# Expert stages of a macaron transformer kernel: three weight sets loaded ahead, five pinned behind the first tile, one-hots by fours

## The chip, the cores and the metric

The kernel runs on one core of one Trainium2 chip. The metric is device microseconds of that core for one execution of the whole program. The engines are named as the profile names them: PE (TensorE, matmuls; PEld is its weight load), DVE (VectorE), ACT (ScalarE), POOL (GpSimd), SP (SyncE, used for issuing DMAs). A name with a q behind it (PEldq, DVEq) stands for what the engine's sequencer does by itself: register loads, semaphore waits, DMA issues.

## The reference

The program is two layers over 1024 tokens of width 512. Cut to what matters here:

```python
h = layernorm(x)                               # 1024 tokens x 512
logits = h @ W_gate + b_gate                   # 8 experts
top2 = the two largest of the 8 logits         # per token
y = sum over its two experts e of
        0.25 * relu(h @ W_e[e] + b_e[e])       # mean of the two, times 0.5
x = x + y
x = x + attention(layernorm(x))                # 32 heads, causal
x = x + y of the same kind                     # expert stage, second time
x = x + 0.5 * lora_ffn(layernorm(x))           # 4 low-rank experts, top 1
x = x + mamba(layernorm(x))                    # 64 heads, state space scan
x = x + 0.5 * lora_ffn(layernorm(x))
```

The expert stage stands twice in the program, once ahead of the attention (called f0) and once after it (f1), with the same weights. Everything is float32, but for the one-hot matrices of the routing, which are bfloat16.

## The kernel before, in words

The tokens lie in eight tiles of 128 (NT = 8). An expert stage is the function `expert_ffn(tag, before_rows, meanwhile, behind_weights)`. It has four parts.

**Loads.** `w_all` (eight experts of 1 MB, 128 partitions by 4 by 512) and `b_all` (eight bias rows, each broadcast over the partitions) are loaded by SP: four experts, their four biases, four experts, their four biases. Then the callback `behind_weights` runs; f0 passes none, in f1 it is the loader of small arrays of the mamba (`par.load`). The loads that follow on SP in f0 are those of the attention's first head group: `w_v`, four of `w_q`, `w_k`, `w_o`. The normalized tokens are written to a DRAM array `rows`, so that they can be gathered.

**Routing.** Logits, the two chosen experts, and for each (token, choice) pair a position `pos` in a list that is ordered by expert and padded to whole tiles of 128 for each expert: NS = 23 slot tiles in the worst case. `ends` says in which slot tile each expert ends. DVE does nearly all of it. Sixteen one-hot matrices `at_row` (128 x 128, line 442) times `what` give, summed on PE into `ps_slot` (line 445), the token of every slot; `lane_of` and `token` (lines 453 and 455) turn this into indices. Apart from that, `past_e` (line 485), two steps `of_f` and the cast `of_i` (line 495) make the number of the expert that each slot tile belongs to, and two casts `slot_i` (line 497) hold where each token finds its two results.

**Slot tiles.** For each of 23 tiles: POOL gathers 128 rows (`xs`, line 463, an indirect DMA that is issued two tiles ahead, from three buffers); PE transposes it (`ps_tr`, line 156) and ACT copies the result (`xt_s`, line 477); PE multiplies it with the weights of one expert (`ps_e`, line 510); DVE adds the bias (`y_e`, line 518), ACT does the relu and issues the store. Which expert it is, is known to the chip alone, so that both PE and DVE read the number from `of_i` into a register:

```python
low, high = max(0, s - (NS - NE)), min(s, NE - 1)
ep = nc.tensor.value_load(of_i[0:1, s : s + 1], min_val=low, max_val=high)   # L506
ev = nc.vector.value_load(of_i[0:1, s : s + 1], min_val=low, max_val=high)   # L507
```

The bound `high` also means that the product of tile s needs the weights of experts 0 to s at most.

**Work beside it.** In f0, POOL makes what the first head group of the attention needs: `w_q` is scaled in two halves (line 659), and four sums and differences of halves of `w_q` and `w_k` (function `sums`, line 636) are formed.

The order of instructions on each engine is not that of the text alone: a scheduler orders them by their dependences, and `tc.keep_in_program_order` pins an instruction to its place in the text. Behind the expert stages, pipelines over the tiles (`Tiles`) run a list of steps, one tile behind the other; a `None` in the list is an empty step, by which the later steps of a tile come one round later. `Lora.steps` is such a list: normalize, transpose, None, gate, choose, turn (which makes `zt`), None, finish.

Of the kernel before, what the change touches and what calls it, by code (L numbers as in the profile page):

```python
# [13 lines left out]
F32 = mybir.dt.float32  # L14
# [4 lines left out]
ALU = mybir.AluOpType  # L19
# [3 lines left out]
P = 128  # L23
# [3 lines left out]
KT = D // P  # L27
# [6 lines left out]

NE = 8
NS = 2 * S // P + NE - 1
NE1 = 4
RANK = 8

# [36 lines left out]
def macaron_kernel(  # L76
# [23 lines left out]
    nc = tc.nc  # L100

    const = ctx.enter_context(tc.tile_pool(name="const", bufs=1))
# [6 lines left out]
    rows = dram.tile([S, D], F32, tag="rows", name="rows")  # L109
    outs = dram.tile([NS * P, D], F32, tag="outs", name="outs")  # L110

# [5 lines left out]

    x = const.tile([P, NT, D], F32, tag="x", name="x")
    hT = const.tile([P, KT, S], F32, tag="hT", name="hT")
    x_src = x_in.rearrange("(t p) d -> p t d", p=P)  # L120
    for t in range(NT):
        (nc.sync, nc.scalar)[t % 2].dma_start(x[:, t, :], x_src[:, t, :])
# [8 lines left out]
    for e in range(NE):  # L131
        nc.gpsimd.memset(rank8[:, e : e + 1], float(NE - e))

    gate_w = const.tile([P, KT, NE], F32, tag="gate_w", name="gate_w")
    nc.scalar.dma_start(gate_w, w_gate.rearrange("(k p) e -> p k e", p=P))
    gate_b = const.tile([P, NE], F32, tag="gate_b", name="gate_b")
    nc.scalar.dma_start(gate_b, b_gate.partition_broadcast(P))
    lg = const.tile([P, NT, NE], F32, tag="lg", name="lg")
    slot = [
        const.tile([P, NT], U32, tag=f"slot{i}", name="slot_i") for i in range(2)  # L140
    ]
# [156 lines left out]
    def expert_ffn(tag, before_rows, meanwhile, behind_weights=lambda: None):  # L298
# [5 lines left out]
        with tc.tile_pool(name=f"{tag}wa", bufs=1) as wap, tc.tile_pool(  # L304
            name=f"{tag}r", bufs=1
        ) as rp, tc.tile_pool(name=f"{tag}w", bufs=3) as wk:
            w_all = wap.tile([P, NE, KT, D], F32, tag="w_all", name="w_all")
            b_all = wap.tile([P, NE, D], F32, tag="b_all", name="b_all")
            for e in range(NE):
                nc.sync.dma_start(  # L310
                    w_all[:, e, :, :], w_e[e].rearrange("(k p) c -> p k c", p=P)
                )
                if e % 4 == 3:
                    for b in range(e - 3, e + 1):
                        nc.sync.dma_start(b_all[:, b, :], b_e[b].partition_broadcast(P))
            behind_weights()


            lanes = rp.tile([P, P], F32, tag="lanes", name="lanes")
            steps = rp.tile([P, NS + 1], F32, tag="steps", name="steps")  # L320
            counts = rp.tile([P, P], I32, tag="counts", name="counts")
            nc.gpsimd.iota(counts, pattern=[[1, P]], base=0, channel_multiplier=0)
            nc.gpsimd.tensor_copy(lanes, counts)
            nc.gpsimd.tensor_scalar(steps, lanes[:, : NS + 1], float(P), None, ALU.mult)
            lane = rp.tile([P, 1], F32, tag="lane", name="lane")
# [63 lines left out]
            ends = rp.tile([P, NE], F32, tag="ends", name="ends")  # L389
# [14 lines left out]
            pos = rp.tile([P, 2, NT], F32, tag="pos", name="pos")  # L404
            for i, sel in enumerate((sel1, sel2)):
# [7 lines left out]
            flat = pos.rearrange("p i t -> p (i t)")  # L413
            past = rp.tile([P, n2, NS + 1], F32, tag="past", name="past_s")
            nc.vector.tensor_tensor(
                past,
                flat.unsqueeze(2).to_broadcast([P, n2, NS + 1]),
                steps.unsqueeze(1).to_broadcast([P, n2, NS + 1]),
                ALU.is_ge,
# [3 lines left out]
            row_of = rp.tile([P, n2], F32, tag="row_of", name="row_of")  # L423
# [15 lines left out]
            at_row = rp.tile([P, n2, P], BF16, tag="at_row", name="at_row")  # L439
            ps = psml.tile([P, 512], F32, tag="ps", name="ps_slot")  # L440
            for j in range(n2):
                nc.vector.tensor_scalar(
                    at_row[:, j, :], lanes, row_of[:, j : j + 1], None, ALU.is_equal
                )
                nc.tensor.matmul(
                    ps[:, : 2 * NS],
                    lhsT=at_row[:, j, :],
                    rhs=what[:, j, :, :].rearrange("p i s -> p (i s)"),
                    start=(j == 0),
                    stop=(j == n2 - 1),  # L450
                )
# [21 lines left out]
            def turn(s):  # L473
                xs = gathered.pop(s)
                ps = transposes(lambda i: xs[:, i * P : (i + 1) * P], KT)
                xt = wk.tile([P, KT, P], F32, tag="xt", name="xt_s")
                nc.scalar.copy(xt.rearrange("p k c -> p (k c)"), ps)
                turned[s] = xt

            for s in range(2):  # L480
# [1 line left out]


            past = rp.tile([P, NS, NE], F32, tag="past_e", name="past")
            nc.vector.tensor_tensor(
                past,
                ends.unsqueeze(1).to_broadcast([P, NS, NE]),
                lanes[:, :NS].unsqueeze(2).to_broadcast([P, NS, NE]),
                ALU.is_le,
            )  # L490
            of = rp.tile([P, NS], F32, tag="of", name="of_f")
            nc.vector.tensor_reduce(of, past, AX.X, ALU.add)
# [1 line left out]
            of_i = rp.tile([P, NS], I32, tag="of_i", name="of_i")  # L494
            nc.vector.tensor_copy(of_i, of)
            for i in range(2):
                nc.vector.tensor_copy(slot[i], pos[:, i, :])
            turn(0)
            for s in range(NS):
                if s + 2 < NS:  # L500
                    gather(s + 2)
                if s + 1 < NS:
                    turn(s + 1)
                xt = turned.pop(s)
# [3 lines that stand above are left out]
                ps = psml.tile([P, 512], F32, tag="ps", name="ps_e")  # L508
                for k in range(KT):
                    nc.tensor.matmul(  # L510
                        ps,
                        lhsT=xt[:, k, :],
                        rhs=w_all[:, bass.ds(ep, 1), k, :].rearrange("p e c -> p (e c)"),
                        start=(k == 0),
                        stop=(k == KT - 1),
                    )
                y = wk.tile([P, D], F32, tag="y", name="y_e")
                nc.vector.tensor_tensor(
                    y,
                    ps,  # L520
                    b_all[:, bass.ds(ev, 1), :].rearrange("p e c -> p (e c)"),
                    ALU.add,
                )
                nc.scalar.activation(y, y, AF.Relu, scale=0.25)
                nc.scalar.dma_start(outs[s * P : (s + 1) * P, :], y)
                if s > 3 and s % 2 == 0 and meanwhile:
                    meanwhile.pop(0)()
# [3 lines left out]
    def collect(make):  # L531


        def f(t):
            pair = pairs[t] = make()
            for i in range(2):
                tc.keep_in_program_order(
                    nc.gpsimd.indirect_dma_start(
                        out=pair[:, i, :],
                        out_offset=None,  # L540
                        in_=outs,
                        in_offset=bass.IndirectOffsetOnAxis(
                            ap=slot[i][:, t : t + 1], axis=0
                        ),
                        bounds_check=NS * P - 1,
                        oob_is_err=True,
                    )
                )

        return f  # L550
# [7 lines left out]
    class Lora:  # L558


        def __init__(self, pool):
            self.store = False
            self.pool = pool
            self.nz = NE1 * RANK
            self.lg_w = pool.tile([P, KT, self.nz + NE1], F32, tag="lg_w", name="lg_w")
            nc.scalar.dma_start(self.lg_w, lora_gate_t.rearrange("(k p) c -> p k c", p=P))
            self.lb_w = pool.tile([self.nz, D], F32, tag="lb_w", name="lb_w")
            nc.scalar.dma_start(self.lb_w, lora_b)
            self.ebias = pool.tile([P, NE1], F32, tag="ebias", name="ebias")
            nc.scalar.dma_start(self.ebias, exp_bias.partition_broadcast(P))  # L570
# [5 lines left out]
        def gate(self, t):  # L576
            narrow_by_columns(t, self.lg_w, self.nz + NE1)

        def choose(self, t):
            nz = self.nz  # L580
            ps = narrow_by_rows(t, nz + NE1)
            lg = self.pool.tile([P, 1, NE1], F32, tag="lg", name="lg1")
            nc.vector.tensor_tensor(lg[:, 0, :], ps[:, nz : nz + NE1], self.ebias, ALU.add)
# [29 lines left out]
        def steps(self):  # L613
            return (
                normalize,
                transpose_h,
                None,
                self.gate,
                self.choose,
                self.turn,  # L620
                None,
                self.finish,
            )
# [43 lines left out]
    def attention(left, causal, first, after):  # L667
        with tc.tile_pool(name="a_v", bufs=2) as vp, tc.tile_pool(
            name="a_qk", bufs=2
        ) as qkp, tc.tile_pool(name="a_p", bufs=3) as pp, tc.tile_pool(  # L670
            name="a_pt", bufs=1
        ) as ptp, tc.tile_pool(name="a_o", bufs=5) as op, tc.tile_pool(
            name="a_s", bufs=5
# [10 lines left out]
                both = pp.tile([P, S], F32, tag="pr", name="pair")  # L684
                return both.rearrange("p (i d) -> p i d", i=2)

            Tiles(collect(pair), None, None, add_pair, transpose_h, None, first_v).flush()


            b11, b12 = hT[:, :2, :512], hT[:, :2, 512:]  # L690
# [316 lines left out]
    def mamba(lora, par):  # L1007
        conv, dsk, nwt, w_dt, dtb, av = par.conv, par.dsk, par.nwt, par.w_dt, par.dtb, par.av
        nct = MI // P
        with ExitStack() as ms:  # L1010
# [13 lines left out]
            with tc.tile_pool(name="m_dt", bufs=1) as dp, tc.tile_pool(  # L1024
                name="m_pair", bufs=3
# [77 lines left out]
                def add_bias(t):  # L1103
# [7 lines left out]
                Tiles(  # L1111
                    collect(pair),
                    None,
                    None,
                    add_pair,
                    *lora.steps()[1:],
                    normalize,
# [360 lines left out]
```

## Time and profile before

| what | value |
|---|---|
| median of 3 runs | 2932.33 us (2929.51 to 2936.05) |
| the profiled execution | 2935.3 us, its span 2933.6 us |
| mean granted clock of PE | 0.978 |
| busy: PE, PEld, DVE, ACT, POOL | 95%, 54%, 60%, 24%, 31% of the span |
| f0 | first bn_stats at 4.34, first gather issued at 43.13, first transpose of a tile at 50.09, last product about 143.5 |
| attention | about 148 to 1605 |
| f1 | routing on DVE from 1613.25, first gather issued at 1628.08, first transpose at 1632.78, last product about 1725 |
| LoRA, mamba, LoRA | 1729 to 2933 |

Times in rows of the profile are microseconds from the start of the span unless marked ns. In a row of the timeline stand the start, the duration, the engine, the line, the operation, output and inputs by their names, the shape, how many instructions of the kind were joined, and in brackets how long the engine had stood idle before it and what ended this. "issue" is time in which the engine waited for nothing that the profile shows, for example because its sequencer was at work on instructions that are not counted as busy.

### The profile page before, as it was taken

Reading aid. Unit: us, or ns where it says so; the run is one execution under the profiler, and the core shown is the slowest. Engines: PE = TensorE matmul, PEld = TensorE weight load, DVE = VectorE, ACT = ScalarE, POOL = GpSimd, SP = SyncE. Lnnn points to the kernel's source line nnn. Section 1 sums busy time; section 2 is a strip of 40 time slices with the busy share of each in tenths; the row PEclk is TensorE's granted clock in tenths of the full one; section 3 lists DMA queues with packets and bytes.
Section 4 is the critical chain, followed back from the end, with each engine's and each line's share of the span. In section 5 each row is a group of like instructions: output and inputs, shape, how many; then the busy total and the mean of one; then the engine's idle time right before and its main releaser. Section 6 shows DMA issues by size and latency. Waiting matters only on the chain.

```text
span 2933.6 us, 30294 instructions
## 1 busy us (share of the span) xinstructions
PE 2800.9 (95%) x11051; PEld 1587.3 (54%) x11051; DVE 1745.8 (60%) x3239; ACT 709.4 (24%) x1381; POOL 898.8 (31%) x733
## 2 busy tenths in 40 slices
PE   5979999999999999999999769899999999999989
PEld 3435666656666666666654334454555555555544
DVE  3146555665656656556564234777776777767673
ACT  1212212231212222212222222422222232222320
POOL 4231112121122212112100230255554545455450
PEclk8989999999999999999999889999999999999999
DMA  8420001010010001001015340233232222223210
GB/s 297 126 72 29 15 15 44 1 44 15 15 44 15 29 15 43 15 15 43 1 36 194 101 122 18 83 101 108 86 108 94 86 98 97 93 87 122 87 44 29
DMA packets 102178, 196.99 MB, mean 67 GB/s; under 512 B 9040, under 2 KB 34800, under 8 KB 102032
## 3 DMA queue, kind: packets, MB, share of 16 engines
q1 hardware_dynamic: 84896, 157.15, 16.1%
q0 software_dynamic: 6240, 20.45, 2.7%
q10 hardware_dynamic: 10896, 17.47, 1.6%
q8 instruction: 89, 1.46, 0.2%
q14 instruction: 57, 0.47, 0.1%
HBM read 176.17 MB, written 18.87 MB: 66 GB/s over the span
## 4 chain that ended last, share of the span: by engine, by line
PE 84%; DVE 6%; POOL 4%; issue 3%; DMA 2%; ACT 0%; POOLq 0%; DVEq 0%; SPq 0%; ACTq 0%
PE ps_in L230 15%; PE ps_m L912 13%; PE ps_o L732 8%; PE ps_s L708 8%; PE ps_tr L156 7%; PE ps_out L1360 6%; PE ps_m L884 6%; PE ps_wo L821 6%; PE ps_e L510 5%; PE ps_y L1308 3%; PE ps_up L241 2%; PE ps_st L1326 1%; DVE xc L1161 1%; DVE e_seg L1265 1%; PE ps_v L241 1%
## 5 line engine op out<-in xcount | busy, mean ns | idle before, releaser
L708 PE MATMUL ps_s<-kT,qT 128*128 128x512 f32 (+3 forms) x768 | 292.8, 488 | 0.1
L732 PE MATMUL ps_o<-pT,v 128*128 128x512 f32 (+3 forms) x768 | 260.4, 489 | 0.0
L753 ACT COPY pT<-ps_tr 128x256 f32<-128x256 f32 (+2 forms) x192 | 91.7, 478 | 647.3 <-PE ps_tr L156 635.5
L722 ACT ACTIVATE pr<-ps_s,nm 128x128 f32<-128x128 f32 (+7 forms) x256 | 190.3, 744 | 238.3 <-DVE nm L719 207.9
L1360 PE MATMUL ps_out<-w_out,yg 128*128 128x512 f32 x512 | 241.1, 615 | 3.0 <-DVE yg L1323 3.0
L230 PE MATMUL ps_in<-hT,w_g 128*128 128x512 f32 x512 | 227.1, 596 | 8.2 <-issue 8.2
L1290 POOL TENSOR_TENSOR cs<-cT,dd 128x1024 f32<-128x1024 f32 x56 | 184.2, 3289 | 161.6 <-PE ps_y L1308 138.8
L230 PE MATMUL ps_in<-hT,w_x 128*128 128x512 f32 x512 | 225.8, 593 | 0.0
L732 PEld LDWEIGHTS ps_o<-pT,v 128*128 128x128 f32 x768 | 144.3, 191 | 145.6 <-issue 99.9
L719 DVE TENSOR_REDUCE nm<-ps_s 128x1 f32<-128x128 f32 (+7 forms) x256 | 192.2, 752 | 3.9
L156 PEld LDWEIGHTS ps_tr<-ident,pr 128*128 128x128 f32 x1152 | 136.9, 142 | 76.1 <-issue 44.8
L156 PE MATMUL ps_tr<-ident,pr 128*128 128x128 f32 x1152 | 171.4, 276 | 4.5 <-DVE pr L724 3.2
L510 PE MATMUL ps_e<-w_all,xt_s 128*128 (+1 forms) x368 | 168.1, 601 | 0.0
L724 DVE TENSOR_SCALAR pr<-pr,sm 128x128 f32<-128x128 f32 (+7 forms) x256 | 162.9, 637 | 7.7 <-DVE sm L723 0.5
L230 PEld LDWEIGHTS ps_in<-hT,w_g 128*128 128x128 f32 x512 | 96.6, 190 | 127.8 <-issue 127.8
L230 PEld LDWEIGHTS ps_in<-hT,w_x 128*128 128x128 f32 x512 | 97.0, 190 | 120.9 <-issue 120.4
L1265 DVE TENSOR_TENSOR_SCAN e_seg<-dd,eye 128x1024 f32<-128x1024 f32 x64 | 152.3, 2380 | 7.7 <-PE ps_y L1308 5.8
L1161 DVE SCALAR_TENSOR_TENSOR xc<-ps_in,conv,xc 128x511 f32<-128x511 f32 (+2 forms) x192 | 141.5, 737 | 17.9 <-ACT xc L1157 17.6
L708 PEld LDWEIGHTS ps_s<-kT,qT 128*128 128x128 f32 x768 | 127.5, 192 | 39.8 <-issue 26.8
L1360 PEld LDWEIGHTS ps_out<-w_out,yg 128*128 128x128 f32 x512 | 94.5, 195 | 98.4 <-issue 98.4
L806 POOL TENSOR_TENSOR so<-oT 128x256 f32<-128x256 f32 x28 | 20.0, 726 | 380.2 <-DVE oT L739 336.7
L1284 POOL TENSOR_TENSOR xw<-xdt,erev 128x512 f32<-128x512 f32 x56 | 58.4, 1043 | 251.6 <-DVE xdt L1278 195.0
(271 smaller groups left out, 4759.2 us busy)
## 6 DMA issues: line engine op xcount, KB each, us to landing
dd<-decay SPq DMA_DIRECT2D x128, 512.0 KB
w_all<-in_w_e_dram SPq DMA_DIRECT2D x16, 1024.0 KB
outs<-y_e ACTq DMA_DIRECT2D x46, 256.0 KB
w_v<-in_wkv_dram SPq DMA_DIRECT2D x8, 1024.0 KB
w_q<-in_wq_dram SPq DMA_DIRECT2D x32, 256.0 KB
w_k<-in_wkv_dram SPq DMA_DIRECT2D x8, 1024.0 KB
w_o<-in_wo_dram SPq DMA_DIRECT2D x8, 1024.0 KB
w_x<-in_in_wt_dram SPq DMA_DIRECT2D x8, 1024.0 KB
```

Of the source, the lines that this page charges most:

```text
L156: nc.tensor.transpose(ps[:, i * P : (i + 1) * P], src(i), ident)
L230: nc.tensor.matmul(ps[:, cols : cols + n], lhsT=w[:, k, c0 : c0 + P], rhs=hT[:, k, t0 : t0 + n], start=(k == 0), stop=(k == KT - 1),)
L510: nc.tensor.matmul(ps, lhsT=xt[:, k, :], rhs=w_all[:, bass.ds(ep, 1), k, :].rearrange("p e c -> p (e c)"), start=(k == 0), stop=(k == KT - 1),
L708: nc.tensor.matmul(ps[:, j : j + m], lhsT=qT[:, qt * P : (qt + 1) * P], rhs=kT[:, j : j + m], start=True, stop=True,)
L719: nc.vector.tensor_reduce(nm, ps[:, :n], AX.X, ALU.max, negate=True)
L722: nc.scalar.activation(pr[:, :n], ps[:, :n], AF.Exp, bias=nm, accum_out=sm)
L732: nc.tensor.matmul(ps[:, lo:512], lhsT=v[:, kb, hh * P : (hh + 1) * P], rhs=pT[:, kb, lo:512], start=(kb == 0), stop=(kb == last),)
L821: nc.tensor.matmul(ps[:, j, :], lhsT=lf[i][k][:, j * P : (j + 1) * P], rhs=rt[i][:, k, :], start=(first and j == 0 and k == 0), stop=(k == 1),
L912: nc.tensor.matmul(ps, lhsT=gr["left"][i][:, k, hh * P : (hh + 1) * P], rhs=right[i][:, k, :], start=(first and k == 0), stop=(last and k ...
L1265: nc.vector.tensor_tensor_scan(e.rearrange("p h l -> p (h l)"), dd[:, 0, :], eye8.rearrange("p h l -> p (h l)"), 0.0, ALU.mult, ALU.add,)
L1290: nc.gpsimd.tensor_tensor(cs, un["cT"][:, tok].unsqueeze(1).to_broadcast([P, HPG, P]), dd[:, 1, :].rearrange("p (h l) -> p h l", l=P), ALU ...
L1360: nc.tensor.matmul(po, lhsT=yg[:, k, :], rhs=w_o[:, k, :], start=(k == 0), stop=(k == 3))
```

## The change

The changed kernel does the following.

1. The loads of `gate_w` and `gate_b` stand ahead of the loads of x on ACT's queue; before, they stood behind.
2. SP loads the weights of three experts (NF = 3), then all eight biases. The weights of the other five experts are loaded from ACT's queue; these loads are pinned behind the transposes and the copy of slot tile 0 (`turn(0)`). The callback `behind_weights` is called twice, behind the first loads and behind the second.
3. The sixteen one-hots are made by four instructions of 128 x 512 in place of sixteen of 128 x 128.
4. `past_e` and the two casts `slot_i` are pinned to their place in the text, behind the first two gathers.
5. `Lora.steps` has one more empty step ahead of `turn`; the step lists of the attention and of the mamba have one fewer.

```diff
+NF = 3
...
+    gate_w = const.tile([P, KT, NE], F32, tag="gate_w", name="gate_w")
+    nc.scalar.dma_start(gate_w, w_gate.rearrange("(k p) e -> p k e", p=P))
+    gate_b = const.tile([P, NE], F32, tag="gate_b", name="gate_b")
+    nc.scalar.dma_start(gate_b, b_gate.partition_broadcast(P))
     x_src = x_in.rearrange("(t p) d -> p t d", p=P)
...
-    gate_w = const.tile([P, KT, NE], F32, tag="gate_w", name="gate_w")
-    nc.scalar.dma_start(gate_w, w_gate.rearrange("(k p) e -> p k e", p=P))
-    gate_b = const.tile([P, NE], F32, tag="gate_b", name="gate_b")
-    nc.scalar.dma_start(gate_b, b_gate.partition_broadcast(P))
...
+            def load_expert(eng, e):
+                return eng.dma_start(
+                    w_all[:, e, :, :], w_e[e].rearrange("(k p) c -> p k c", p=P)
+                )
+
+            for e in range(NF):
+                load_expert(nc.sync, e)
             for e in range(NE):
-                nc.sync.dma_start(
-                    w_all[:, e, :, :], w_e[e].rearrange("(k p) c -> p k c", p=P)
-                )
-                if e % 4 == 3:
-                    for b in range(e - 3, e + 1):
-                        nc.sync.dma_start(b_all[:, b, :], b_e[b].partition_broadcast(P))
+                nc.sync.dma_start(b_all[:, e, :], b_e[e].partition_broadcast(P))
             behind_weights()
...
             for j in range(n2):
-                nc.vector.tensor_scalar(
-                    at_row[:, j, :], lanes, row_of[:, j : j + 1], None, ALU.is_equal
-                )
+                if j % 4 == 0:
+                    four = [P, 4, P]
+                    nc.vector.tensor_tensor(
+                        at_row[:, j : j + 4, :],
+                        lanes.unsqueeze(1).to_broadcast(four),
+                        row_of[:, j : j + 4].unsqueeze(2).to_broadcast(four),
+                        ALU.is_equal,
+                    )
...
-            nc.vector.tensor_tensor(
-                past,
-                ends.unsqueeze(1).to_broadcast([P, NS, NE]),
-                lanes[:, :NS].unsqueeze(2).to_broadcast([P, NS, NE]),
-                ALU.is_le,
+            tc.keep_in_program_order(
+                nc.vector.tensor_tensor(
+                    past,
+                    ends.unsqueeze(1).to_broadcast([P, NS, NE]),
+                    lanes[:, :NS].unsqueeze(2).to_broadcast([P, NS, NE]),
+                    ALU.is_le,
+                )
             )
...
             for i in range(2):
-                nc.vector.tensor_copy(slot[i], pos[:, i, :])
+                tc.keep_in_program_order(nc.vector.tensor_copy(slot[i], pos[:, i, :]))
             turn(0)
+            for e in range(NF, NE):
+                tc.keep_in_program_order(load_expert(nc.scalar, e))
+            behind_weights()
             for s in range(NS):
...
                 self.gate,
                 self.choose,
+                None,
                 self.turn,
...
-            Tiles(collect(pair), None, None, add_pair, transpose_h, None, first_v).flush()
+            Tiles(collect(pair), None, add_pair, transpose_h, None, first_v).flush()
...
                 Tiles(
                     collect(pair),
                     None,
-                    None,
                     add_pair,
                     *lora.steps()[1:],
```

More of the change, by code (lines that the diff above doesn't have):

```diff
@@ L308, in expert_ffn @@
             b_all = wap.tile([P, NE, D], F32, tag="b_all", name="b_all")
-            for e in range(NE):
-                nc.sync.dma_start(
+            def load_expert(eng, e):
+                return eng.dma_start(
                     w_all[:, e, :, :], w_e[e].rearrange("(k p) c -> p k c", p=P)
                 )
-                if e % 4 == 3:
-                    for b in range(e - 3, e + 1):
-                        nc.sync.dma_start(b_all[:, b, :], b_e[b].partition_broadcast(P))
+            for e in range(NF):
+                load_expert(nc.sync, e)
+            for e in range(NE):
+                nc.sync.dma_start(b_all[:, e, :], b_e[e].partition_broadcast(P))
             behind_weights()
```

## The prediction

> **What bounds the kernel now.** I read first the page's busy shares, then the chain of waits inside the two expert stages, then the timeline and the windows there, because all edits lie in those stages.
>
> ```profile
> PE 2800.9 (95%) x11051; PEld 1587.3 (54%) x11051; DVE 1745.8 (60%) x3239; ACT 709.4 (24%) x1381; POOL 898.8 (31%) x733
> ...
> L510 PE MATMUL ps_e<-w_all,xt_s 128*128 (+1 forms) x368 | 168.1, 601 | 0.0
> ```
>
> TensorE (PE) is busy 95% of the span: whatever makes PE stand still is paid in full, and of its 133 us of idleness 58 lie in the two expert stages (f0 from 0 to 148 us: 38; f1 from 1605 to 1633: 20) and 26 behind the second (1726 to 1765). Its L510 groups run without gaps once begun (idle 0.0). Second, the chain of waits in f1:
>
> ```profile
> 1611.27 16.57 issue
> 1627.84 0.03 POOLq L463
> 1627.87 0.21 issue
> 1628.08 3.50 DMA xs<-rows,token
> 1631.58 1.20 issue
> 1632.78 1.96 PE ps_tr L156 x8
> ```
>
> The rows of the first tile had landed at 1631.58, yet PE began only at 1632.78. The "issue" of 1.20 us is PE's own sequencer, and the rows of line 506 (`value_load` of `of_i` on PE) in that stretch say what it did:
>
> ```profile
> L506 PEldq TENSOR_LOAD <-of_i x18: 296/299/307, 1620.3 to 1632.1; - x18
> L506 PEldq FUSED_REGOPS  x18: 146/146/151, 1620.7 to 1632.5; - x18
> L506 PEldq SEQ_ASSERT  x18: 18/18/18, 1620.9 to 1632.7; - x18
> ```
>
> Each register load is three sequencer instructions. 18 of them fill 1620.3 to 1632.7, so one takes 12.4 / 18 = 0.69 us (0.30 + 0.15 + 0.02, the rest between them). They are executed in program order with the matmuls. Before the change they cost little because they stand where PE waits for routing and gathers anyway. DVE pays the same price: the 13.93 us "issue" before the first `y_e` below are such loads, and nobody on PE waits for it.
>
> Third, f0 in the timeline:
>
> ```profile
> 43.13 1.27 POOL L463 DMA_INDIRECT xs<-rows,token  x1 [25.85 <-DMA b_all<-in_b_e_dram]
> ...
> 50.09 2.15 PE L156 MATMUL ps_tr<-ident,xs 128*128 128x128 f32 x8 [8.19 <-DMA xs<-rows,token]
> ...
> 52.56 2.78 POOL L659 TENSOR_SCALAR w_q<-w_q 128x1024 f32<-128x1024 f32 x1
> ...
> 56.76 0.69 DVE L518 TENSOR_TENSOR y_e<-ps_e,b_all 128x512 f32<-128x512 f32 x1 [13.93 <-issue]
> ...
> 67.93 2.37 POOL L636 TENSOR_TENSOR sqk<-w_q,sqk 128x1024 f32<-128x1024 f32 x1
> ...
> 74.06 0.63 PE L156 MATMUL ps_tr<-ident,xs 128*128 128x128 f32 x4 [1.85 <-DMA xs<-rows,token]
> ```
>
> The first gather is issued at 43.13 and used at 50.09: 7.0 us, against 3.5 in f1, because the DMA engines are full. The 1.85 at 74.06 is a gather that was queued on POOL behind the attention's weight sums (L636). The windows of f0 give the clock and the traffic (columns: PE, PEld, DVE, ACT, POOL busy, then PEclk, DMA share, GB/s):
>
> ```profile
> 44.00:48.00 4.00, 0.00 (x0) 0.00 (x0) 0.00 (x0) 0.00 (x0) 2.42 (x3) 0.50 1.19 314
> 52.00:54.00 2.00, 2.00 (x5) 0.97 (x4) 0.00 (x0) 0.59 (x1) 1.93 (x2) 0.50 1.05 387
> 54.00:56.00 2.00, 2.00 (x5) 0.85 (x5) 0.00 (x0) 0.00 (x0) 1.73 (x2) 0.95 1.01 376
> 56.00:60.00 4.00, 4.00 (x14) 1.91 (x12) 0.69 (x1) 1.11 (x2) 3.85 (x3) 1.00 0.49 164
> ```
>
> After some 8 us without work PE's granted clock is 0.50, and it is back at 1.00 about 4 us after work resumed. At 0.50 a pass of the expert product takes 0.85 us, at 1.00 0.43. f1 shows the same after 5.9 idle us (0.50 at 1632 to 1636).
>
> **The change, part by part.** The instruction order of the two built programs was compared; what follows rests on it.
>
> *PE's register loads, both stages.* With `past_e` pinned behind the gathers, `of_i` comes after `token` on DVE, so the loads can no longer stand among the `ps_slot` matmuls. In the changed program PE has: all `ps_slot`, 3 loads, transposes of tile 0, 1 load, transposes of tile 1, `ps_e` of tile 0, transposes of tile 2, then 19 loads in a row, then `ps_e` of tile 1. Count from T, the first transpose. The transposes of tile 2 wait for the third gather, which POOL issues 2.9 us after the first (43.13, 46.02): they leave the sequencer at about T + 2.7. 19 x 0.683 (the 18 loads' cadence without the ones that shared it with matmuls) = 13.0, so `ps_e` of tile 1 starts at T + 15.7. By T + 6.2 the array has finished all it had (1.9 of transposes, 3.4, 0.9), so it idles 9.5 us and the clock falls to 0.50, as in the window above: four passes take 4 x 0.85 = 3.4 and the transposes 0.9. `ps_e` of tile 2 starts at T + 20.0. Before: 56.99 - 50.09 = 6.9 in f0 and 1640.25 - 1632.78 = 7.5 in f1. Loss: 13.1 in f0, 12.5 in f1. If the clock stayed up, 2.1 less each; if tile 2 is dispatched earlier, 0.7 less. Range 10 to 14 each.
>
> *Five 1 MB loads on ACT.* They are pinned after the first `xt_s` copy, so the second copy, and behind it the first relu and its store, wait for five issues. SP's row of four such issues in f1 before shows 2.35 us (1570.33); the next four, into a loaded queue, took 7.25. Five lie between 2.9 and 9; I take 6. That ends at about T + 8, plus a copy of 0.6, under the register loads that end at T + 15.7: nothing is added. Without that cover `ps_e` of tile 1 would come 2 to 6 us late in each stage. Expert 3 is needed first at T + 24: the five have landed by then (5.2 MB at 0.37 MB per us is 14 us from T + 2).
>
> *First gather of f0.* SP now issues x, three weight sets, eight biases, then the attention's `w_v`, `w_q`, `w_k`. POOL's built order has the two `w_q` scalings and the four sums ahead of the first gather: 2 x 2.78 + 4 x 2.38 = 15.1 us. They start when half of `w_q` has landed: x 2.1 + weights 3.1 + biases 2.1 + rows written 2.1 + `w_v` 1.0 + `w_q` 0.5 = 11 MB at 0.37 MB per us (mean of the windows from 28 to 56) from 2.5 us on, so at about 32. `w_k` lands at 36, in time for the sums. Gather at 32 + 15.1 = 47.3. POOL may be slowed by DVE's routing beside it: the nearest row is the mamba's `cs`, the same shape as the sums, 2345 ns at least and 3527 in the median there, with DVE busy, against 2377 for a sum in f0. One stretched instruction adds 1, all until routing ends up to 4; I take 1: gather at 48.3. DMA is then quiet, since experts 3 to 7 come later, so landing takes f1's 3.5: T at 51.9, +1.7 against 50.09 (-3 to +7).
>
> ```profile
> L636 POOL TENSOR_TENSOR sqk<-w_k x1: 2405/2405/2405, 59.6 to 59.6; 128x1024 f32<-128x1024 f32 x1
> ...
> L1290 POOL TENSOR_TENSOR cs<-cT,dd x56: 2345/3527/4422, 1843.1 to 2855.1; 128x1024 f32<-128x1024 f32 x56
> ```
>
> The Trainium skill (SBUF — State Buffer, "Who interferes with whom") speaks against the change here: a DVE instruction with two SBUF inputs and a GpSimd instruction that reads SBUF lock each other out for a whole instruction, and the one-hots become exactly such instructions. By that rule some 5 us of DVE's two-input routing work, an estimate, would be added to POOL's 15.1, and the sum below would end 4 us higher. The `cs` row agrees in kind, not in proof: it stretched by about half.
>
> What this order gains in f0: with the sums done, the stall at 74.06 goes, -2.05 (68.61 to 74.53 less the cadence of 3.87). Gate weights first: PE waits 2.7 us for `gate_w` near 12 us, worth perhaps 1 of it on the gate's path, since the x tiles arrive 1.7 us apart; routing then ends earlier, but POOL decides: zero.
>
> *Routing, f1.* `token` comes earlier: six small DVE instructions move behind it, 0.6 in all; 16 one-hots of 3.22 become 4 of about 0.69 (the row of `y_e`, same shape), 2.8, so 0.4; `ps_slot` no longer interleaves with loads, 1.3 (the last four groups stand 0.7 apart, at the loads' cadence); a DVE register load between `lane_of` and `token` goes, 0.45. Sum 2.75. No loads hold tile 0, another 1.2. T is 3.9 earlier (3 to 5). Five loads that PE had later in the stage go, 0.3. POOL has no sums in f1. The mamba's small loads are issued twice, 2.2 us on SP that end at 1562, 8 us before SP's wait for the weights' buffer ends (1570.33): zero.
>
> *Pipelines behind the stages.* One empty step moves in each: the LoRA after f1 has its transpose of `zt` a step later, where PE waits 2.5 and 2.7 us for it; -1 (-4 to +2).
>
> Sum: f0 +1.7 + 13.1 - 2.0 = +12.8; f1 -3.9 + 12.5 - 0.3 = +8.3; behind -1: +20. The profiled execution took 2935.3 us (span 2933.6), 3 above the median of 2932.33; +20 on the median is 2952.
>
> **Rivals.**
> *Loads hidden, faster.* If PE's sequencer ran far enough ahead, the 19 loads would lie under matmuls: then 1.7 - 2.0 - 3.9 - 0.3 - 1 = -5.5, 2927. Place: between tile 2's transposes and tile 1's product. It decides only if 13 us of work is queued there; there are about 3.5 us. For it: DVE's 14 us of loads were hidden. Against: the 1.20 us above, with only the end of a run of loads.
> *ACT's queue decides.* Loads hidden as above, but the five issues hold the second copy: 2.2 to 6.4 a stage, -5.5 + 4.4 to 12.8: 2931 to 2940.
> *POOL later.* `w_q` lands at 35 or the sums stretch by half: 4 to 8 more, 2956 to 2960. For it: SP's issues of `w_q` stood 1.1 to 2.0 us each in f0.
> *The change doesn't do what it says.* One-hots by fours handle as many elements, and the earlier gate is hidden: both are worth about nothing in f0; that is in the sum.
>
> **How the numbers follow.** Forecast 0.72, POOL later 0.14, ACT decides 0.08, loads hidden 0.06. What a measurement of this kernel can tell from no change is about 0.2%, 5.9 us. The first two are slower; ACT's case lies mostly within; hidden loads straddle the bound downwards. Low end: both stalls at 10, the clock up, T of f0 3 earlier, gives about 2940; high end: POOL later with 14 each, 2961.
>
> **What would show it.** Right: in both stages one gap of 9 to 10 us in PE, called "issue", before `ps_e` of tile 1, with 19 rows of register loads in it and PEclk 0.50 after; L636 ahead of the first gather in f0; gather to use 3.5 us; T of f1 3 to 5 us earlier. Wrong: no such gap, or one that ends with ACT's copy, or a first gather before 43 or after 53.

## The result and the profile after

The changed kernel takes 2950.97 us in the median of 6 runs (2945.11 to 2955.64), the kernel before 2931.84 in 6 runs beside it: +19.1 us, ratio 1.0059 with the interval 1.0049 to 1.0069. The forecast was 2952 (2940 to 2961). The profiled execution took 2949.5 us, its span 2946.9; against the profile of before (2933.6) that is only +13.3. The two profiles lie on opposite sides of their medians (3.5 above, 1.5 below), so sums over traces are compared with 13.3, not with 19.1.

On the page PE is busy 95% again, with the same number of instructions in a longer span:

```profile
span 2946.9 us, 30270 instructions
...
PE 2799.2 (95%) x11051; PEld 1585.7 (54%) x11051; DVE 1754.6 (60%) x3215; ACT 709.1 (24%) x1381; POOL 898.7 (30%) x733
```

The start of f0 in the timeline (start, duration, engine, line, operation, in brackets the idle time before and its end):

```profile
35.51 5.70 POOL L674 TENSOR_SCALAR w_q<-w_q 128x1024 f32<-128x1024 f32 x2 [16.18 <-DMA w_q<-in_wq_dram]
...
48.81 2.33 POOL L651 TENSOR_TENSOR sqk<-w_q,sqk 128x1024 f32<-128x1024 f32 x1
...
51.33 1.27 POOL L472 DMA_INDIRECT xs<-rows,token  x1 [0.19 <-DVE slot_i L508]
...
55.06 1.11 PE L157 MATMUL ps_tr<-ident,xs 128*128 128x128 f32 x4 [10.43 <-DMA xs<-rows,token]
...
56.22 7.82 ACTq L312 DMA_DIRECT2D w_all<-in_w_e_dram  x5
...
64.07 0.59 ACT L486 COPY xt_s<-ps_tr 128x512 f32<-128x512 f32 x1 [7.28 <-DMA w_all<-in_w_e_dram]
...
71.51 6.26 PE L524 MATMUL ps_e<-w_all,xt_s 128*128 x8 [8.90 <-issue]
```

POOL's scalings wait for `w_q` until 35.51; the six instructions of the attention end at 51.14, and only then goes the first gather out, though the tokens that it reads were ready at 45.07. PE transposes tile 0 at 55.06 (before: 50.09). ACT's five issues hold its second copy until 64.07; but the product of tile 1 comes at 71.51, and what PE waited for is "issue", its own sequencer, 8.90 us. The row of line 520, the register loads, in f1 (least, median and greatest duration in ns, first and last start), where the first transpose is at 1639.56 and the product of tile 1 at 1657.53:

```profile
L520 PEldq TENSOR_LOAD <-of_i x23: 296/299/485, 1636.9 to 1656.6; - x23
```

All 23 now lie between `of_i` and the product of tile 1. The windows in f0 (PE, PEld, DVE, ACT, POOL busy, PEclk, DMA share, GB/s):

```profile
64.00:68.00 4.00, 0.00 (x0) 0.00 (x0) 0.00 (x0) 1.59 (x3) 0.00 (x0) 0.81 1.05 401
68.00:72.00 4.00, 0.49 (x1) 0.50 (x2) 0.00 (x0) 0.00 (x0) 0.00 (x0) 0.50 1.04 383
72.00:76.00 4.00, 4.00 (x6) 1.44 (x5) 0.00 (x0) 0.00 (x0) 0.00 (x0) 0.50 0.78 292
```

PE stands still through 64 to 71.5, its clock falls to 0.50 within that time, and the product of tile 1 pays for it: 6.26 us in place of 3.60.

One reading needs care. In f1 the chain of waits names another cause:

```profile
1642.38 15.00 DMA w_all<-in_w_e_dram
1657.38 0.14 issue
1657.53 2.90 PE ps_e L524 x3
```

It puts PE's start, after 10.81 us of idleness, down to a weight load of an expert that landed at 1657.38. That is a coincidence of two ends. The sequencer came to the product 0.80 us after the start of its last register load in f1 (1656.62 to 1657.42) and as much in f0 (70.61 to 71.41), where no transfer ended. The second and third experiments settle it.

### The profile page after: what moved, and what is told of

Same layout as the page of the kernel before. It is cut to its first block, busy times and chain, and to the rows that moved or that the text cites. A ratio compares the mean times of both kernels' runs of the same rounds, so it can differ in the third digit from the quotient of the medians.

```text
span 2946.9 us, 30270 instructions
## 1 busy us (share of the span) xinstructions
PE 2799.2 (95%) x11051; PEld 1585.7 (54%) x11051; DVE 1754.6 (60%) x3215; ACT 709.1 (24%) x1381; POOL 898.7 (30%) x733
## 4 chain that ended last, share of the span: by engine, by line
PE 84%; DVE 7%; POOL 4%; issue 2%; DMA 2%; ACTq 0%; ACT 0%; POOLq 0%; SPq 0%; DVEq 0%
PE ps_in L231 15%; PE ps_m L927 13%; PE ps_o L747 8%; PE ps_s L723 8%; PE ps_tr L157 7%; PE ps_out L1374 6%; PE ps_m L899 6%; PE ps_wo L836 6%; PE ps_e L524 5%; PE ps_y L1322 3%; PE ps_up L242 2%; PE ps_st L1340 1%; DVE xc L1175 1%; DVE e_seg L1279 1%; PE ps_v L242 1%
## 5 line engine op out<-in xcount | busy, mean ns | idle before, releaser
L524 PE MATMUL ps_e<-w_all,xt_s 128*128 (+1 forms) x368 | 171.3, 610 | 19.7 <-DMA w_all<-in_w_e_dram 10.8
L532 DVE TENSOR_TENSOR y_e<-ps_e,b_all 128x512 f32<-128x512 f32 x46 | 31.8, 691 | 183.8 <-PE ps_e L524 183.8
L674 POOL TENSOR_SCALAR w_q<-w_q 128x1024 f32<-128x1024 f32 x16 | 44.4, 2777 | 304.5 <-DMA w_q<-in_wq_dram 303.9
```

The source lines that it names most:

```text
L524: nc.tensor.matmul(ps, lhsT=xt[:, k, :], rhs=w_all[:, bass.ds(ep, 1), k, :].rearrange("p e c -> p (e c)"), start=(k == 0), stop=(k == KT - 1),
```

## The experiments

The theory (A): the run of 19 register loads is what costs, about 12 us in each stage, and ACT's block of five issues lies under it. The rival (R1): ACT's block is the hold, and the loads only fill it. The run is made when the program is built, not on the chip: with each edit undone by itself, it goes if ACT's loads are not in one block or if `past_e` is not pinned (then 6 of the loads stay in a row). Putting back the gate's loads, the one-hots or the empty steps leaves it in place. The likely reason, argued and not shown: the scheduler counts ACT's five issues as time in which PE would idle, and fills that time with loads.

**1. `past_e` and `slot_i` left to the scheduler.**

```diff
-            tc.keep_in_program_order(
-                nc.vector.tensor_tensor(past, ...)
-            )
+            nc.vector.tensor_tensor(past, ...)
```

> The changed kernel with past_e and slot_i left to the scheduler again. In its built order 15 register loads stand before the first transpose and 6 in a row before the product of tile 1, in place of 19. Theory A (the run of 19 loads is what costs; ACT's five DMA issues lie under it): in both stages PE's hold before the product of tile 1 is cut to what ACT's issues leave, second copy ended at T + 9.7 in f0 and T + 8.4 in f1 (T: first transpose), about -9.5 and -11 with the clock staying up; f1's routing is 3 longer again; median about 2934 (2930 to 2938). Rival R1 (ACT's five issues are the hold and the loads only fill it): PE's product of tile 1 starts as late as in the changed kernel, 2951 plus 3 for routing, 2954.

Measured: 2933.21, ratio to before 0.9998 (0.9989 to 1.0008), 18 below the changed kernel. R1 had 2954 and falls here. (In the trace 17 loads, not the 15 expected, stand ahead of the first transpose, and six ahead of the product of tile 1, which comes 9.6 and 8.2 us after the first transpose.)

**2. Register loads one per tile, ACT's block kept.**

```diff
-                ep = nc.tensor.value_load(of_i[0:1, s : s + 1], ...)
+                with tc.issue_after(mms[s - 2].ins) if s > 2 else nullcontext():
+                    ep = nc.tensor.value_load(of_i[0:1, s : s + 1], ...)
```

> The changed kernel with each PE register load of tile 3 and on issued behind the product two tiles before, so one load per tile; ACT's five issues stay in one block. Theory A: product of tile 1 starts at T + 9.7 (f0) and T + 8.4 (f1), released by ACT's second copy, in place of T + 16.5 and T + 18.0; with the clock staying at 1.0 that is -9.5 and -11: median about 2931 (2928 to 2935). Rival R1 (ACT is the hold): 2951, within 3.

Measured: 2929.62, ratio 0.9983 (0.9974 to 0.9993). The timeline of f0, first transpose at 56.06:

```profile
57.22 7.25 ACTq L312 DMA_DIRECT2D w_all<-in_w_e_dram  x5
...
64.51 0.59 ACT L486 COPY xt_s<-ps_tr 128x512 f32<-128x512 f32 x1 [6.70 <-PE ps_tr L157]
...
65.14 3.70 PE L525 MATMUL ps_e<-w_all,xt_s 128*128 x8 [1.36 <-ACT xt_s L486]
```

The same five issues take nearly as long as in the changed kernel (7.25 for 7.82), and PE waits 1.36 us for the copy behind them. The product of tile 1 comes 9.1 us after the first transpose, not 16.5, at full clock. The weights of f1 are loaded as in the changed kernel too, and its product of tile 1 comes at 8.2 in place of 18.0, released by the copy: the transfer that the chain named was not the hold.

**3. ACT's five loads one per tile.**

```diff
-            for e in range(NF, NE):
-                tc.keep_in_program_order(load_expert(nc.scalar, e))
...
                     turn(s + 1)
+                if NF + s < NE:
+                    tc.keep_in_program_order(load_expert(nc.scalar, NF + s))
```

> The changed kernel with ACT's five weight loads issued one per slot tile (expert 3 + s behind the copy of tile s + 1) in place of five in a row. Its built order has PE's register loads one per tile by itself: the run of 19 is the scheduler's, which fills the time that it takes for ACT's block. Theory A: both holds are gone, product of tile 1 at T + 7 in both stages, -12.2 and -12.1, median about 2927 (2923 to 2931), and 3 to 5 below the kernel with only the loads spread, which is what ACT's block costs without cover. Rival R2 (the weights' own transfers beside the gathers are what holds PE): products of tiles 3 and on wait for DMA, 2935 or more.

Measured: 2926.19, ratio 0.9979 (0.9969 to 0.9988): 24.8 below the changed kernel, and below the second experiment by 3.4 in the medians, though by 1.2 only in the ratios, so their difference in time is not well fixed. The product of tile 1 comes at 7.1 after the first transpose in both stages, and all products of a stage together wait 0.3 and 0.4 us for weights, so R2 falls. Undoing one property of the change, the block, takes away more than its whole loss.

**4. The pin alone (`past_e` and `slot_i`), on the kernel before.**

```diff
-            nc.vector.tensor_tensor(past, ...)
+            tc.keep_in_program_order(
+                nc.vector.tensor_tensor(past, ...)
+            )
```

> The kernel before with past_e and slot_i pinned as in the change, nothing else. Built order: no loads among ps_slot, 3 before the first transpose, one per tile later, no run. Theory A: f1's first transpose comes 4 earlier and nothing is lost, f0's token 2 earlier with DMA as full as before: median about 2926 (2923 to 2929). Rival R3 (the pin itself makes the run of loads): +18, about 2950.

Measured: 2925.65, ratio 0.998 (0.9969 to 0.999). The pin is a gain by itself: without ACT's block in the program, the loads are built one per tile. In f0 four of them lie up to 48.3, and the first transpose of f0 comes at 48.27 (before: 50.09). In f1 it comes 16.1 us after the start of the routing, in place of 19.5.

**5. The gate's loads first, on the kernel before.**

```diff
+    nc.scalar.dma_start(gate_w, ...)
+    nc.scalar.dma_start(gate_b, ...)
     for t in range(NT):
         (nc.sync, nc.scalar)[t % 2].dma_start(x[:, t, :], x_src[:, t, :])
```

> The kernel before with the gate's two loads ahead of the loads of x, nothing else. In the changed kernel's trace the third and fourth x loads of ACT's queue stood at 3.71 and 6.84 us (before: 1.7 and 2.2), and the second x tile was read at 8.51 in place of 4.95. Theory B (gate loads first delay x by more than they save): PE's wait of 2.7 for gate_w goes, but the logits end 1.9 later, and with POOL free the first gather is later by as much: 2935 (2933 to 2937), first transpose about 52. Rival R4, the forecast's own term (a microsecond of the wait saved): 2932, first transpose about 49.

Measured: 2935.34 against 2933.52, ratio 1.0004 (0.9994 to 1.0013), which the times don't tell from no change. The trace does:

```profile
1.84 4.18 ACTq L126 DMA_DIRECT2D x<-in_x_dram  x4
...
8.10 1.29 DVE L162 BATCH_NORM_STATS2 ln_st<-x 128x6 f32<-128x512 f32 x2 [3.02 <-DMA x<-in_x_dram]
```

ACT's four x loads take 4.18 us to be issued, where they took 1.86 (in the trace the last two wait for the semaphores of the gate's two loads), and DVE waits 3.02 for the second tile. The first transpose of a gathered tile is at 52.10, 2.0 later. In the traces theory B holds and R4 falls: in all seven kernels here that load the gate first the last logits of f0 come between 29.48 and 30.51, in the four that load it behind x between 27.82 and 28.96.

**6. The empty steps, on the kernel before.**

```diff
                 self.choose,
+                None,
                 self.turn,
...
-            Tiles(collect(pair), None, None, add_pair, ...)
+            Tiles(collect(pair), None, add_pair, ...)
```

and one `None` fewer in the mamba's list.

> The kernel before with the moved empty steps (one more ahead of turn, one fewer in the attention's and the mamba's lists), nothing else. Theory C: the changed kernel's trace gained 4.2 us between 1750 and 1765 and 1.3 at the end of the program from this edit alone: 2928 (2925 to 2930). Rival R5, the forecast's term: -1, 2932.

Measured: 2926.09 against 2933.52, ratio 0.9971 (0.9958 to 0.9984), that is -7.4, more than theory C's -5.5. The waits of PE behind f1, first in the kernel before, then in this one:

```profile
PE ps_zt L598 <- DVE ln_mv L164: 2.7, 1, 2.7
PE ps_zt L598 <- DVE ln_rs L149: 2.4, 1, 2.4
```

```profile
PE ps_tr L156 <- DVE lg L583: 1.2, 2, 1.0
...
PE ps_zt L598 <- DVE ln_mv L164: 0.3, 1, 0.3
```

The transpose of `zt` had stood in front of other work of PE and waited 5.1 us; a step later it waits 0.3, though other small waits stand in its place. In the trace PE stands 1.1 us later than before at the end of f1 and 4.2 earlier at 1800, so 5.3 are gained there; 1.4 more come by 1900 and 2.9 at the end of the program, and these were not taken apart.

**7. POOL's sums of f0 behind the gathers, on top of experiment 3.**

```diff
-            first["left"] = left_of_heads(first, left, later)
+            made = []
+            first["left"] = left_of_heads(first, left, made)
+            later.extend(lambda f=f: tc.keep_in_program_order(f()) for f in made)
```

> The kernel with ACT's loads one per tile, and POOL's two scalings and four sums of f0 pinned to their place in the text (one every second slot tile from tile 4 on), so behind the first gathers. Theory D (the first gather of f0 waits for POOL's 15 us, and DVE's two-input routing work is held up by the same sums): first gather at about 42 in place of 53, first transpose at about 46: -10, 2917 (2913 to 2920). Rival R6 (routing or transfers would hold the first gather to 50 anyway, or the sums come too late for the attention): 2924 or more.

Measured: 2918.32, ratio 0.9946 (0.9929 to 0.9962).

```profile
38.09 2.49 DVE L448 TENSOR_TENSOR at_row<-lanes,row_of 128x512 bf16<-128x512 f32 x4
...
41.71 1.27 POOL L472 DMA_INDIRECT xs<-rows,token  x1 [22.79 <-DVE past L495]
...
45.38 1.11 PE L157 MATMUL ps_tr<-ident,xs 128*128 128x128 f32 x4 [4.41 <-DMA xs<-rows,token]
```

The first transpose comes at 45.38 in place of 56.64; the median falls by 7.9, the ratio by 0.0033 (10 us), the span of the profile by 11.2. The first gather did wait for POOL, but by two ways. In the changed kernel the tokens were ready at 45.07 and the gather was queued on POOL behind the sums until 51.14. In experiment 3 the sums ended at 51.33, and the gather waited on for the routing until 53.01, because the same sums had stretched DVE's one-hots to 11.12 us (rows under experiment 9; 2.49 here).

**8. The gate's loads put back, on top of experiment 7.**

```diff
-    nc.scalar.dma_start(gate_w, ...)   # ahead of x
...
+    nc.scalar.dma_start(gate_w, ...)   # behind x, as before
```

> As the kernel with POOL's sums late, and the gate's loads put back behind those of x. Theory B with D: another 1.9 earlier in f0, 2915 (2911 to 2918), below both kernels compared. Rival R4 (gate first is a gain or nothing): 2917 to 2918.

Measured: 2916.07 (2913.39 to 2916.95), ratio 0.9936 (0.992 to 0.9953). The first transpose comes at 44.92, only 0.5 earlier: of the 1.9 expected most is missing (the last logits come at 28.96 for 29.48; on average over the kernels named in experiment 5 the two orders lie 1.4 apart), and the difference in time is within the scatter. It is the fastest version here, 17.5 below the kernel before and 35 below the changed one.

**9. The one-hots by sixteen, on top of experiment 3, one run.**

```diff
-                if j % 4 == 0:
-                    nc.vector.tensor_tensor(at_row[:, j : j + 4, :], ...)
+                nc.vector.tensor_scalar(
+                    at_row[:, j, :], lanes, row_of[:, j : j + 1], None, ALU.is_equal
+                )
```

> The kernel with ACT's loads one per tile, with the sixteen one-hot instructions of 128 x 128 (tensor with a scalar column) back in place of the four of 128 x 512 (two tensors). Theory E (a DVE instruction with two tensors from SBUF and POOL's sums lock each other out for whole instructions, one-input ones pass): in f0 the one-hots take about 3.2 us in all beside the sums, in place of 11.1, and the sums lie close together and end near 50.7, so that the first gather goes out at about 51, 2 earlier than 53.0; in f1, without sums, they take 3.2 in place of 2.5. Rival R7 (DVE is slowed beside POOL whatever its inputs): the one-hots stretch to 6 us or more in f0 and the gather stays at 53.

Measured: 2928.84 in one run. The one-hots and POOL's sums in f0, first in experiment 3, then in this one:

```profile
40.76 11.12 DVE L448 TENSOR_TENSOR at_row<-lanes,row_of 128x512 bf16<-128x512 f32 x4
...
45.79 2.79 POOL L651 TENSOR_TENSOR w_k<-w_q,w_k 128x1024 f32<-128x1024 f32 x1
...
53.01 1.27 POOL L472 DMA_INDIRECT xs<-rows,token  x1 [1.68 <-DVE past L495]
```

```profile
40.54 11.68 DVE L446 TENSOR_SCALAR at_row<-lanes,row_of 128x128 bf16<-128x128 f32 x16
...
53.23 1.27 POOL L467 DMA_INDIRECT xs<-rows,token  x1 [3.25 <-DVE past L490]
```

Theory E falls. DVE gets about one instruction in for each of POOL's sums, with two tensors or with one: the longest single one-hot took 2451 ns here, against a median of 278. So the number of inputs is not what decides between these two forms; R7 told the result, the stretch and the gather at 53. The sums did end early, at 49.98 as theory E had it, but the gather then waited 3.25 us more for the routing. Why the form with one tensor is held as well, no run shows.

## Why the prediction was right, step by step

**Register loads, the main term.** Right in place, cause and size, but not by clean working. The gap in PE was 8.90 us in f0 and 10.81 in f1 (forecast 9 to 10); in f1 the profile does not call it "issue". Tile 2's transposes left the sequencer 3.2 us after the first transpose in f0 and 4.4 in f1 (forecast 2.7; in f1 the third gather took 5.1 us beside the weight loads, not 3.5). The 19 loads took 13.2 and 13.4 (13.0). The clock fell to 0.50. The product of tile 1 started at T + 16.5 and T + 18.0 (15.7). Here lies a slip of the forecast: a tile's product is eight passes, not four, and the rows at 56.99 and 1640.25 that it took for tile 2 are tile 1. To 15.7 it added 4.3 for four slow passes and the transposes, and set that against 6.9, the start of tile 1 before. With the right tile its own numbers give 15.7 - 6.9 = 8.8, and the slow product adds 2.7 (6.26 less 3.60, as measured): 11.5 in f0; it wrote 13.1. Measured from transpose to the product of tile 2, the loss is 12.2 in f0 (23.0 against 10.8) and 12.05 in f1 (23.4 against 11.3). The slip (1.6 too much in f0, 2.7 in f1) and the later start of the product (0.8 and 2.3) went against each other, which was luck.

**ACT's block.** Forecast: six us, under the loads, 2 to 6 us a stage without that cover. It took 7.8 and 6.5, added nothing, and without the cover it costs 2.0 in f0 and 1.1 in f1 (experiment 2 against 3). What the forecast did not see is that the block made the run of loads: it took the order as built for given, and priced the two apart.

**First gather of f0.** Right that POOL's 15 us stand ahead; too small: +1.7 forecast, +5.0 measured. The term that failed is the landing of `w_q`, 35.5 in place of 32: between 2.5 and 35.5 the loads moved 0.352 MB per us, not 0.37, and 11.6 MB, not 11. POOL was slowed by 0.5 only (15.6 for 15.1, forecast 1). The lock that the Trainium skill states (SBUF — State Buffer, "Who interferes with whom") did show, but DVE was the side that lost: four one-hots took 4.64 us here and 11.1 in experiment 3, against 2.49 in f1, where POOL had no sums. The forecast had priced that rule on POOL. The traces bear it out for POOL's sums, not for its scalings of `w_q`, which read SBUF too: in the changed kernel three of the four one-hots, with two inputs each, ran beside the second scaling one behind the other at their 0.68 us (39.60 to 41.48), and only the fourth, beside a sum, took 2.83. Here the measurement decides.

**Gate weights first.** Forecast a gain of about 1, hidden. Hidden it was, but it is a loss: the last logits came at 29.75 in place of 27.82. Its reason, x tiles that arrive 1.7 us apart, is not in the trace of before: there the eight tiles landed in pairs, all by 8.9.

**Gather stall and f1's routing.** The stall at 74.06 went: products follow each other by 3.87 from 78.05 on. f1's routing began 10.8 later and its first transpose 6.8 later: 4.0 gained, forecast 3.9, and from the parts that it named: 2.8 from the start of the routing to `token` (forecast 2.75), 1.2 from there to the transpose (1.2).

**Behind the stages.** -1 forecast with -4 to +2; in the trace it is -4.2 by 1900 (of it -5.3 by 1800, as in experiment 6) and -1.3 at the end, and experiment 6 puts it at -7.4, beyond the range. This is the worst-sized term. The two waits of 2.5 and 2.7 that the forecast names were the answer: they add to 5.1 (2.7 and 2.4 in the view above), and nearly all of it went.

**Clock.** No term. Through the attention the trace of after gains 4.4 us, and most of it is the clock. 1.3 come right behind f0, where the first product with `w_v`, eight passes with about the same waits ahead of them, takes 4.55 us in place of 6.05: the clock is 0.68 over 180 to 184 in the trace of after, 0.50 over 165 to 169, the same work, in that of before. The edit of the attention's list is not the cause: experiment 6 has it and takes 6.15, experiment 5 lacks it and takes 4.72. 0.8 come in small steps. 2.3 come at 1561 to 1566, where PE's instructions are the same. There two waits of PE for the softmax, 3.2 us in all in both executions, stand ahead of a clock of 0.50 in the one and of 1.00 in the other. Windows of the same work, before first, then after:

```profile
1560.00:1565.00 5.00, 4.21 (x11) 2.74 (x12) 1.34 (x2) 0.68 (x2) 0.78 (x3) 0.50 0.14 36
```

```profile
1573.00:1578.00 5.00, 3.96 (x15) 2.29 (x16) 1.35 (x2) 0.84 (x2) 0.63 (x3) 1.00 0.45 112
```

The last 16 passes there, the attention's product with `v`, take 5.86 us in six of the eleven profiles of this record and 7.1 to 7.8 in five, the kernel before among them, whatever the edit.

So the two profiles add up: f0 +15.1, attention -4.4, f1 +8.0, behind -5.5, together 13.2 of 13.3. Against the forecast's +12.8, +8.3 and -1, f0 was 2.3 too low and the pipelines 4.5 too high: that the total of 20 lies so close to the medians' 19.1 owes something to errors of both signs.

## What to carry to other kernels

Instructions that a sequencer executes itself, such as register loads, are not in the busy time of an engine: read the order of the built program for runs of them, and price each run at its cadence against the work queued ahead of it. A block of DMA issues on a compute engine can change the order that a scheduler chooses for other engines, as here; issue them one per step of the loop, and ask of each early load what other load it pushes back. A change of five parts can hide gains of several us behind one bad part, so test each part alone on the kernel before.

## What was not expected of the hardware

A register load costs 0.68 us on PE's sequencer (299, 146 and 18 ns for its three instructions, the rest between them), a sixth of a slot tile of 3.87. Five 1 MB loads issued back to back block their engine for 6.2 to 7.8 us. While POOL formed sums of 128 x 1024 from SBUF, DVE's one-hots came through one per sum, some 2.3 to 2.8 us apart, where they take 0.2 (128 x 128) or 0.6 (128 x 512) each by themselves. Beside POOL's scaling they went through. Other work of DVE differed by its kind: beside a sum in f0 of the changed kernel the cast `of_i` took 2.26 us, 0.18 in f1, and the reduce `of_f` 0.34 in both. And two waits of 3.2 us in all may or may not be followed by a clock of 0.50, so that the same instructions differ by 2 us between two profiles.
